# A two-step graph layer on one core: products of the nodes made in the prologue, interleaved keys, lists as a stream, VectorE in text order

## The chip, the core and the metric

The kernel runs on one core of one Trainium2 chip. The metric is device time in microseconds (us); the runs of a kernel are compared by their medians. PE is TensorE (PEld its weight loads), DVE is VectorE, ACT is ScalarE, POOL is GpSimd, SP is SyncE, on whose queue most transfers are issued. L730 is line 730 of the kernel.

## The reference

A graph layer over N = 3327 nodes with 256 features. The matrix `adj` is 3327 x 3327 with about four nonzero entries beside the diagonal in a row.

```python
def _top_p_attention(X, W1, W2, W3):          # 64 wide
    q = X @ W1.T @ W2.T
    k = X @ W3.T
    probs = softmax(q @ k.T)
    ...                                       # keep each row's largest until their sum reaches 0.9
    return A / A.sum(-1, keepdims=True)

h = relu(layernorm(x))
R = adj + eye(N);  R = R / R.sum(-1, keepdims=True)
Z = 0;  Xf = Xa = X = h
for n in range(2):
    A = _top_p_attention(Xa, W1, W2, W3)
    Xf = R @ Xf
    Xa = A @ Xa
    Z = Z + Xf @ U1[n].T + Xa @ U2[n].T
out = x + layernorm(h + Z)
```

## The kernel before

The nodes are cut into NT = 26 tiles of 128 rows. All of h stays on chip (`x0`), as do the keys and queries of a step. A **prologue** makes them: per tile the layer norm, a transposition, and `prep`, which makes keys (L476), rows for moments (L478) and the matrix gsum (L487), in 12 PE instructions of the profile (a matmul of 32-bit numbers is two of them).

Then each of the two steps goes over the 26 tiles, row block by row block, in a software pipeline. For one tile:

- `weights` (L541, L545): logits against all keys in four quarters, exponentials on ACT into a buffer e of 128 x 3328. Its last column goes by way of POOL (L552). `project` (L506 to L525) makes the queries, and on POOL the tile's law, from moments over all keys.
- `measured`: the threshold of the 0.9 mass is guessed from the law and the sum, then corrected by whole passes of ACT over e (L590, 3.08 each), two in step 0 and three in step 1, with small operations on ACT, DVE and POOL between them.
- `settle`: DVE only. The values under the guess (L652), their largest by 20 MAX operations (L656), five or six rounds on the candidates (L661, L663), and the cut itself (L673).
- `Sums.turn` and `Sums.sum`: e is transposed on PE (L717), copied by ACT (L719), and multiplied with the nodes on PE (L730). The last copy (L737) gives the attention row xa.
- `listed`, `packed`, `gathered` (step 0): the nonzero blocks of a row block of `adj`. Seven loads by SP are reduced by DVE (L747), 26 block maxima become a list (L748 to L759); a list's leftovers are packed over the partitions (L764, L777), and POOL gathers five blocks of `adj` (L788) and five of the nodes (L797) by index. In step 0 the blocks are stored (cx) and in step 1 loaded again.
- `spread`: PE multiplies these (L805), which gives Xf; step 1 adds its product at once (L897).
- `first_end` (step 0): the row's Xf and Xa are transposed (L466) and multiplied with U1 and U2 of both steps (L821, L824, L834, 256 wide), since in step 1 R·(Xf U1) and A·(Xa U2) can be summed directly; then `prep` for step 1. `finish` (step 1): the closing layer norm (L842 to L852).

`PLAN` is a table of letters: in each round i of a step, seven parts; each letter advances one piece of a tile's work (m measured, w weights, s spread, e first_end, l lists, f finish), and a part of the sum closes each. `LATE` shifts the sums by parts. At the end PE's and ACT's instructions are tied in the order of this text; DVE's, POOL's and SP's order is left to a scheduler, which sorts by its own model. In round i, settle belongs to tile i, measured to i + 1, weights to i + 2, the sums to i - 1.

`prove` sets a flag where a guess missed, and an exact search behind this code runs only if it is set.

The lists of before stand in the rounds as follows:

```python
for i in range(-3, NT + 2):
    t = i - 1
    if valid(i):
        settle(step, i, live[step, i])
```

```python
def index_next(t):
    if valid(t + 3):
        over[t + 3] = listed(t + 3)
```

Of the kernel before, what the change touches and what calls it, by code (L numbers as in the profile page):

```python
# [9 lines left out]
F32 = mybir.dt.float32  # L10
# [294 lines left out]


# [17 lines left out]
AHEAD = (1, 2)  # L324
CUT = 4
# [13 lines left out]
def guess_graph_layer(ctx, tc, x, adj, w1t, w2t, w3t, u1t, u2t, ln_g, ln_b, out, flag):  # L339
# [22 lines left out]
    x0 = nodes.tile([P, NT, D + 1], F32, tag="x0", name="x0")  # L362
# [10 lines left out]
    for t0 in range(0, NT, 2):  # L373
        nc.sync.dma_start(
            x0[:, t0 : t0 + 2, :D], x[t0 * P : (t0 + 2) * P].rearrange("(t p) d -> p t d", p=P)
        )
# [11 lines left out]
    u1 = const.tile([P, 2, ND, D], F32, tag="u1", name="u1")  # L388
    u2 = const.tile([P, 2, ND, D], F32, tag="u2", name="u2")
    gam = const.tile([P, D], F32, tag="gam", name="gam")  # L390
    bet = const.tile([P, D], F32, tag="bet", name="bet")
    for n in range(2):
        nc.scalar.dma_start(u1[:, n], u1t[n].rearrange("(c p) e -> p c e", p=P))
        nc.scalar.dma_start(u2[:, n], u2t[n].rearrange("(c p) e -> p c e", p=P))
    nc.scalar.dma_start(gam, ln_g.to_broadcast([P, D]))
    nc.scalar.dma_start(bet, ln_b.to_broadcast([P, D]))
    G.memset(x0[:, :, D : D + 1], 1.0)
    for e in es[:4]:
        G.memset(e[:, N:NP], 0.0)
    half = const.tile([P, 2], F32, tag="half", name="half")  # L400
    G.memset(half[:, :1], -0.5)
    G.memset(half[:, 1:], 0.5)
# [26 lines left out]
    ends = const.tile([P, NT], F32, tag="ends", name="ends")  # L429
    index = const.tile([P, NT, DIRECT + 1], I32, tag="index", name="index")  # L430
    hx = dram.tile([P, NT, D + 1], F32, tag="hx", name="hx")
# [29 lines left out]
    def transposed(rows, pt=None):  # L461

        if pt is None:
            pt = ps_t.tile([P, 4, P], F32, tag="pt", name="pt")
        for c in range(ND):
            PE.transpose(pt[:, c, :], rows[:, c * P : (c + 1) * P], ident)  # L466
        xT = tpool.tile([P, ND, P], F32, tag="xT", name="xT", bufs=2)
        S.copy(xT, pt[:, :ND, :])
        return xT


    def prep(step, xT, t):
        h, j = divmod(t, HALF)
# [10 lines left out]
        S.copy(qry[qp, j, :], pk[qp, 0, :])  # L484
        yield
# [6 lines left out]
    def moments(step):  # L492
        gs = small.tile([DA, DA + 1], F32, tag="gs", name="gs", bufs=1)
        V.tensor_scalar(gs, gsum[:, step, :], 1.0 / N, None, ALU.mult)
# [7 lines left out]
    def project(step, t):  # L502
        h, j = divmod(t, HALF)
        qp = slice(DA, P) if h == 0 else slice(0, DA)
        pq = ps_t.tile([P, 4, P], F32, tag="pt", name="pq")
        PE.matmul(pq[:, 0, :], w2d[qp, :], qry[qp, j, :], start=True, stop=True)  # L506
        pr_ = pq[:, 1:3, :].rearrange("p a b -> p (a b)")[:, : 2 * DA + 2]
        PE.matmul(pr_, qry[qp, j, :], qm[qp, step, :], start=True, stop=True)
        qT = tpool.tile([P, P], F32, tag="qT", name="qT", bufs=2)
        S.copy(qT, pq[:, 0, :])  # L510
        mq = small.tile([P, 2 * DA + 2], F32, tag="mq", name="mq", bufs=2)
        S.copy(mq, pr_)
# [8 lines left out]
        G.tensor_tensor(col(2), col(1), half[:, 1:], ALU.pow)  # L521
# [6 lines left out]
    def weights(step, t, live):  # L528

        qT, ms = project(step, t)  # L530
        yield
        e = es[(2, 3, 0, 1, 4, 5)[t % 6] if step else t % 4]
        za = small.tile([P, CUT + 1], F32, tag="za", name="za")
        w = HALF * P
        wd = w // CUT
        for n in range(CUT):
# [11 lines left out]
            else:  # L548
                S.activation(e.rearrange("p (a n) -> p a n", a=2)[:, :, c : w - 1], pl[:, :, : wd - 1],
                             AF.Exp, accum_out=za[:, n : n + 1])  # L550
                S.activation(za[:, n + 1 :], pl[:, 0, wd - 1 : wd], AF.Exp)  # L551
                G.tensor_copy(e[:, w - 1 : w], za[:, n + 1 :])  # L552
        live[step, t] = dict(e=e, za=za, ms=ms, Z=rec[:, step, 3, t : t + 1])
# [5 lines left out]
    def measured(step, r):  # L559
        e, za, ms, Z = r["e"], r["za"], r["ms"], r["Z"]  # L560

        g = small.tile([P, 20], F32, tag="g", name="g")
        r["col"] = col = lambda k: g[:, k : k + 1]
        con = lambda k: one[:, k : k + 1]
        S.activation(za, za, AF.Copy, accum_out=Z)
        S.activation(col(0), Z, AF.Ln)
# [3 lines left out]
        S.activation(col(9), col(3), AF.Exp, scale=ms[:, 3:4], bias=ms[:, 8:9])  # L573
        S.activation(col(4), col(2), AF.Square, bias=con(4))
# [5 lines left out]
        G.tensor_scalar(col(5), col(1), OFFSET[step], None, ALU.mult)  # L580
        if step == 0:
            G.tensor_scalar(col(10), col(9), col(5), 1.0, ALU.mult, ALU.add)
        else:
            G.tensor_scalar(col(14), col(9), 0.25, None, ALU.mult)
        yield
        oa = small.tile([P, 3], F32, tag="oa", name="oa")

        def through(k, f, guess, sign):
            ja = scan.tile([P, NP], U8, tag="ja", name="ja")
            S.activation(ja, e, f, bias=guess, scale=sign, accum_out=oa[:, k : k + 1])  # L590

        through(0, AF.Relu, col(9), -1.0)
        yield
        through(1, AF.Sign, col(12), 1.0)
# [4 lines left out]
        if step == 0:  # L599
            S.activation(col(3), col(4), AF.Square, scale=col(1), bias=con(1))  # L600
            S.activation(col(3), col(3), AF.Ln, scale=0.5, bias=col(10))
            S.activation(col(3), col(3), AF.Identity, scale=-1.0, bias=col(6))
            S.activation(col(3), col(3), AF.Exp, scale=col(11))

            V.tensor_scalar(col(5), oa[:, 1:2], 31.0 - NP, BIG, ALU.is_lt, ALU.mult)
            V.tensor_scalar(col(6), col(4), col(1), 0.35, ALU.mult, ALU.is_lt)
            V.scalar_tensor_tensor(col(5), col(6), BIG, col(5), ALU.mult, ALU.add)
            V.tensor_scalar(col(3), col(3), 1.0e20, col(9), ALU.min, ALU.mult)
            V.tensor_tensor(col(16), col(3), col(5), ALU.add)
            return  # L610
# [405 lines left out]
```

## Time and profile before

| what | value |
|---|---|
| median of 3 runs | 1583.5 us (1581.93 to 1588.3) |
| the profiled execution's own time | 1581.76 us |
| its span in the trace | 1580.0 us |
| busy PE, DVE, ACT, POOL | 88%, 75%, 76%, 53% |
| mean granted TensorE clock | 0.94 |
| step 0, first to last L652 | 115.00 to 837.12 us |
| step 1, first to last L652 | 925.34 to 1527.24 us |

Busy time is an average over stages with different limits, so the stages are read apart: prologue, step 0 with lists, step 0 without, the boundary, step 1, the tail. The granted clock (1.00 is full) tells how fast PE ran in a stage. A row of the chain or of a timeline names engine, line, operation, output and inputs; in brackets stands the idle time ahead of it and what ended it.

### The profile page before, as it was taken

The numbers are of one execution on the slowest core, as the hardware profiler recorded it, in microseconds if no ns is written. First come the engines' busy times: TensorE is split into PE (matmuls) and PEld (weight loads), VectorE is DVE, ScalarE is ACT, GpSimd is POOL, SyncE is SP. The second block draws the span as 40 slices with busy tenths as digits, with TensorE's granted clock in tenths as the row PEclk, the third lists the DMA queues.
The fourth block names the chain that finished last, engine by engine and source line by source line (L and its number), as shares of the span: only waits on it lengthen the run. The fifth ranks groups of instructions, "written<-read, shape, count | busy, mean of one in ns | idle before, by whom it ended". The sixth has DMA issues, their size and how long they took to land.

```text
span 1580.0 us, 23741 instructions
## 1 busy us (share of the span) xinstructions
PE 1389.4 (88%) x6923; PEld 1056.5 (67%) x6923; DVE 1186.5 (75%) x3910; ACT 1203.3 (76%) x2758; POOL 830.6 (53%) x1336
## 2 busy tenths in 40 slices
PE   5967999989999999999999639899989898999885
PEld 4745677767776767777778426676666666766674
DVE  4349887888788777576675058988988889889883
ACT  5457777675776767777774399999999899999961
POOL 6625655456556546556561316556555465565532
PEclk9566999999999999999999859999999999999998
DMA  7623444444545422212221201122121221221210
GB/s 227 174 84 102 129 148 137 139 138 137 156 124 149 138 73 66 65 59 56 61 69 60 61 0 54 58 80 61 61 81 52 69 61 61 80 61 61 80 44 20
DMA packets 86460, 139.64 MB, mean 88 GB/s; under 512 B 14737, under 2 KB 49296, under 8 KB 86320
## 3 DMA queue, kind: packets, MB, share of 16 engines
q1 hardware_dynamic: 67168, 93.76, 19.0%
q0 software_dynamic: 16640, 42.69, 10.1%
q10 hardware_dynamic: 2512, 1.57, 0.3%
q8 instruction: 57, 0.93, 0.2%
q14 instruction: 83, 0.68, 0.1%
HBM read 114.10 MB, written 23.87 MB: 87 GB/s over the span
## 4 chain that ended last, share of the span: by engine, by line
PE 34%; DVE 28%; ACT 16%; DMA 10%; POOL 7%; issue 4%; SPq 0%; POOLq 0%; ACTq 0%; DVEq 0%
PE pa L730 15%; DMA at<-in_adj 7%; ACT ja L590 6%; DVE e L673 5%; DVE cand L656 5%; PE pt L717 5%; PE pr L805 4%; POOL xg L797 4%; PE pl L541 4%; DVE fm L747 4%; DVE w L652 4%; DMA ac<-cx 2%; ACT e L545 2%; PE pk L476 2%; DVE x L673 1%
## 5 line engine op out<-in xcount | busy, mean ns | idle before, releaser
L730 PE MATMUL pa<-xw,eT 128*128 128x256 f32 x1352 | 332.9, 388 | 32.1 <-ACT xa L737 32.1
L719 ACT COPY eT<-pt 128x512 f32<-128x512 f32 (+1 forms) x364 | 202.6, 557 | 190.5 <-PE pt L717 190.5
L730 PE MATMUL pa<-x,eT 128*128 128x256 f32 x1352 | 334.9, 389 | 0.0
L590 ACT ACTIVATE ja<-e,g 128x3328 uint8<-128x3328 f32 x106 | 326.5, 3080 | 0.0
L730 PEld LDWEIGHTS pa<-xw,eT 128*128 128x128 f32 x1352 | 250.2, 191 | 112.5 <-ACT xa L737 41.2
L730 PEld LDWEIGHTS pa<-x,eT 128*128 128x128 f32 x1352 | 255.4, 194 | 34.9 <-issue 1.2
L541 PE MATMUL pl<-k,qT 64*128 64x416 f32 x832 | 210.4, 597 | 51.2 <-ACT qT L510 47.9
L656 DVE MAX8 cand<-w 128x8 f32<-128x168 f32 (+1 forms) x1040 | 248.4, 317 | 0.0
L788 POOL DMA_INDIRECT ac<-in_adj,index x130 | 187.3, 1441 | 97.6 <-DVE index L782 65.4
L717 PE MATMUL pt<-ident,e 128*128 128x128 f32 x1144 | 180.9, 279 | 23.7 <-DVE e L673 9.5
L717 PEld LDWEIGHTS pt<-ident,e 128*128 128x128 f32 x1144 | 140.7, 142 | 66.8 <-ACT xw L835 18.5
L747 DVE TENSOR_REDUCE fm<-at 128x4 f32<-128x512 f32 (+1 forms) x182 | 116.0, 642 | 87.3 <-DMA at<-in_adj 86.7
L673 DVE SCALAR_TENSOR_TENSOR e<-e,rec 128x3328 f32<-128x3328 f32 x44 | 164.3, 3733 | 1.3
L652 DVE SCALAR_TENSOR_TENSOR w<-e,g 128x3328 f32<-128x3328 f32 x44 | 162.1, 3684 | 1.5
L797 POOL DMA_INDIRECT xg<-vx,index x130 | 131.1, 1009 | 54.6 <-issue 34.6
L805 PE MATMUL pr<-xg,ac 128*128 128x257 f32 (+1 forms) x520 | 141.5, 395 | 20.7 <-DVE s L897 20.7
L797 POOL DMA_INDIRECT xg<-hx,index x130 | 127.3, 979 | 35.0 <-issue 32.0
L541 PEld LDWEIGHTS pl<-k,qT 64*128 64x128 f32 x832 | 70.3, 199 | 98.8 <-ACT qT L510 49.6
L552 POOL COPY e<-za 128x1 f32<-128x1 f32 x44 | 21.3, 485 | 212.3 <-ACT za L551 212.3
L545 ACT ACTIVATE e<-pl 128x832 f32<-128x832 f32 x132 | 113.6, 865 | 13.7 <-PE pl L541 13.7
L805 PEld LDWEIGHTS pr<-xg,ac 128*128 128x128 f32 x520 | 90.0, 193 | 35.8 <-DVE s L897 25.0
L577 POOL TENSOR_SCALAR g<-g 128x1 f32<-128x1 f32 x52 | 55.6, 1069 | 84.0 <-ACT g L573 84.0
(217 smaller groups left out, 2326.3 us busy)
## 6 DMA issues: line engine op xcount, KB each, us to landing
at<-in_adj SPq DMA_DIRECT2D x156, 256.0 KB, 3.0
cx<-ac SPq DMA_DIRECT2D x26, 384.0 KB, 2.4
ac<-cx SPq DMA_DIRECT2D x26, 384.0 KB, 3.2
hx<-x SPq DMA_DIRECT2D x26, 128.5 KB, 3.0
x<-in_x SPq DMA_DIRECT2D x13, 256.0 KB, 5.3
at<-in_adj SPq DMA_DIRECT2D x26, 128.0 KB, 2.2
xr<-in_x SPq DMA_DIRECT2D x26, 128.0 KB, 2.2
vx<-sv SPq DMA_DIRECT2D x26, 128.0 KB, 2.1
```

Source lines behind the costliest of these rows:

```text
L541: PE.matmul(pl[:, a, :wd], qT[p, :], keys[step][p].rearrange("p a b -> p (a b)")[:, c : c + wd], start=True, stop=True)
L590: S.activation(ja, e, f, bias=guess, scale=sign, accum_out=oa[:, k : k + 1])
L652: V.scalar_tensor_tensor(w, e, col(16), e, ALU.is_lt, ALU.mult, accum_out=d2)
L656: V.max(cand[:, 8 * s : 8 * s + 8], w[:, s * SEG : min(NP, (s + 1) * SEG)])
L673: V.scalar_tensor_tensor(e, e, at(1), e, ALU.is_ge, ALU.mult, accum_out=ra)
L717: PE.transpose(pt[:, j, :], e[:, (j0 + j) * P : (j0 + j + 1) * P], ident)
L719: S.copy(eT[:, :w, :], pt[:, :w, :])
L730: PE.matmul(self.pa, eT[:, j - 4 * k, :], self.xa[:, j, :D], start=j == 0, stop=j == NT - 1)
L747: V.tensor_reduce(fm[:, j0 : j0 + n], at[:, :n], AX.X, ALU.max, apply_absolute_value=True)
L788: G.indirect_dma_start(out=ac[:, k, :], out_offset=None, in_=rows, in_offset=bass.IndirectOffsetOnAxis(ap=index[:, t, k : k + 1], axis=0), ...
L797: G.indirect_dma_start(out=xg[:, k, :w], out_offset=None, in_=rows, in_offset=bass.IndirectOffsetOnAxis(ap=index[:, t, k : k + 1], axis=0))
L805: PE.matmul(pr[:, :w], ac[:, k, :], own if k == KT - 1 else xg[:, k, :w], start=k == 0, stop=k == KT - 1)
```

## The change

1. **Products once.** The product of h with U1 of both steps (512 wide) is made in the prologue by a new `products`, 11 tiles there and the rest in the first two rounds, and stored in `ax` (step 0's half) and `bx` (step 1's half, with a column of ones). R is applied to these rows instead of to h: `spread` of step 0 diffuses `bx`, adds `ax` scaled, and stores `vx` itself. `first_end` keeps only xa's transposition and one 512-wide product with U2.
2. **Interleaved keys.** Tile t of keys lies at column block t // 2 of half t % 2. So three quarters of the key columns need only the first tiles, and the weights of tiles 0 to 2 of each step are begun before the last keys are there: in the prologue, and in rounds 24 to 26 of step 0. The moments leave the last tiles uncounted.
3. **Lists as a stream.** `listed` becomes one generator over all tiles, a unit being one load with its reduce: two units per prologue tile from t = 6, then six per round.
4. **Order of DVE.** `settle` is cut into seven pieces, with letters d (and c, n for the pieces carried into the next round); the new letters a, p, g stand for lists, packing and gathering. DVE's instructions are now tied in text order too. LATE is one part larger in both steps.
5. **Step 1's measurement.** Eight small ACT operations between the passes go; some of their work moves to DVE, more to POOL; DVE's small operations after the third pass fall from 13 to 8 in all. The last column's exponential is written and summed by ACT itself.

```diff
-        h, j = divmod(t, HALF)
+        j, h = divmod(t, 2)
...
-                S.activation(za[:, n + 1 :], pl[:, 0, wd - 1 : wd], AF.Exp)
-                G.tensor_copy(e[:, w - 1 : w], za[:, n + 1 :])
+                S.activation(e[:, w - 1 : w], pl[:, 0, wd - 1 : wd], AF.Exp, accum_out=za[:, n + 1 :])
...
+        V.tensor_scalar(col(3), oa[:, 1:2], float(NP), col(7), ALU.add, ALU.mult)
+        V.tensor_scalar(col(4), col(3), oa[:, 0:1], 0.0, ALU.subtract, ALU.max)
...
+        G.tensor_scalar(col(12), col(4), d1, col(1), ALU.subtract, ALU.mult)
+        G.tensor_scalar(col(8), col(8), col(12), None, ALU.mult)
+        G.tensor_scalar(col(12), col(12), col(12), 1.0e-12, ALU.mult, ALU.add)
+        G.tensor_tensor(col(12), col(12), half[:, 2:], ALU.pow)
+        G.tensor_scalar(col(12), col(12), col(8), 0.7, ALU.mult, ALU.max)
+        G.tensor_scalar(col(11), col(12), 1.5, col(11), ALU.min, ALU.mult)
...
-    def first_end(t, xf, xa):
-        fT = transposed(xf)
-        yield
-        aT = transposed(xa)
+    def first_end(t):
+        aT = transposed(live.pop(("r", t)))
         yield
         pz = ps_r.tile([P, 2 * D], F32, tag="pr", name="pz")
...
         for c in range(ND):
-            PE.matmul(pz[:, D:], fT[:, c, :], u1[:, 1, c, :], start=c == 0, stop=c == ND - 1)
-        sv = row.tile([P, 2 * D], F32, tag="sv", name="sv", bufs=2)
-        S.copy(sv, pz)
-        nc.sync.dma_start(vx[:, t, :], sv[:, D:])
...
+            PE.matmul(pz, aT[:, c, :], u2[:, c].rearrange("p n d -> p (n d)"), start=c == 0, stop=c == ND - 1)
+        S.copy(xw[:, t, :], pz[:, D:])
...
+    def products():
+
+        for t in range(NT):
+            pool, tag = ((ps_a, "pa"), (ps_r, "pr"))[t % 2]
+            pz = pool.tile([P, 2 * D], F32, tag=tag, name="pz")
+            for c in range(ND):
+                PE.matmul(pz, hT[:, t, c, :], u1[:, c].rearrange("p n d -> p (n d)"),
+                          start=c == 0, stop=c == ND - 1)
+            u = uh[:, t % 4, :]
+            (V.tensor_copy if t < EARLY[1] else S.copy)(u[:, : 2 * D], pz)
+            nc.sync.dma_start(ax[t], u[:, :D])
+            nc.sync.dma_start(bx[:, t, :], u[:, D:])
+            yield
...
+        if t >= 6:
+            run(lister, 2)
+            if t % 2 == 0:
+                run(product, 1)
...
+        own = row.tile([P, D + 1], F32, tag="own", name="own", bufs=2)
+        nc.sync.dma_start(*((own[:, :D], vx[:, t, :]) if step else (own, bx[:, t, :])))
+        s1 = row.tile([P, D], F32, tag="s1", name="s1", bufs=4)
+        nc.sync.dma_start(s1, (sx if step else ax)[t])
...
         V.scalar_tensor_tensor(s1, pr[:, :D], rr, s1, ALU.mult, ALU.add)
-        live["f", t] = s1
...
+        if step == 0:
+            nc.sync.dma_start(vx[:, t, :], s1)
...
-    PLAN = (("mwsss", "lmsss", "ewl", "wee", "mee", "mwel", "we"),
-            ("mwss", "lms", "ww", "mssf", "mw", "msf", "mw"))
-    LATE = (0, 3)
...
+    PLAN = (("mdwsssa", "mdsssa", "ewpda", "wsda", "mpdea", "mwedga", "wmdeg"),
+            ("cmwss", "cnms", "wwnfd", "mdsss", "smwdfg", "mdfg", "mwdf"))
+    LATE = (1, 4)
...
-    for engine in (PE.engine, S.engine):
+    for engine in (PE.engine, S.engine, V.engine):
```

What this does to the order is seen at three places. First DVE in step 0, before, ahead of one tile's settle: the reduces of a list (L747) and its small operations stand in one clump between the operations that end `measured` (L605 to L609).

```order
L747 TENSOR_REDUCE fm<-at 128x2
L747 TENSOR_REDUCE fm<-at 128x4
L748 SCALAR_TENSOR_TENSOR fm<-fm,back 128x26
L749 MEMSET fm 128x1
L751 MAX lists<-fm 128x8
L752 MATCH_REPLACE fm<-lists,fm 128x26
L754 TENSOR_SCALAR index<-lists 128x4
L753 MAX lists<-fm 128x8
L747 TENSOR_REDUCE fm<-at 128x4 x2
L605 TENSOR_SCALAR g<-oa 128x1
L828 TENSOR_TENSOR sv<-sv,x_95 128x256
L747 TENSOR_REDUCE fm<-at 128x4 x2
```

The same engine and step now, inside a settle (L708 to L727 are its rounds and its cut; the settle of the next tile is L696):

```order
L881 TENSOR_TENSOR sv<-pz,x_95 128x256
L800 TENSOR_REDUCE fm<-at 128x4
L723 SCALAR_TENSOR_TENSOR e_101,ra<-e_101,rec 128x3328
L724 RECIPROCAL ra<-ra 128x1
L800 TENSOR_REDUCE fm<-at 128x4
L626 TENSOR_SCALAR g<-oa 128x1
```

The reduces (now L800) stand singly between long operations, and the end of `measured` comes after the cut.

Second, DVE in step 1, before, from the cut (L673) to the next tile's settle: the small operations after the third pass (L628 to L641) come in one row behind the cut.

```order
L673 SCALAR_TENSOR_TENSOR x_95,ra<-x_95,rec 128x3328
L675 TENSOR_TENSOR cum<-dr,bb 128x48
L674 RECIPROCAL ra<-ra 128x1
L897 SCALAR_TENSOR_TENSOR s_11542<-pr,rrs,s_11542 128x256
L676 TENSOR_REDUCE rec<-cum 128x1
L628 TENSOR_SCALAR g<-g 128x1
L629 TENSOR_TENSOR g<-g 128x1
L630 TENSOR_SCALAR g<-g 128x1
L639 TENSOR_SCALAR g<-g 128x1
L631 TENSOR_SCALAR g<-g 128x1
L632 RECIPROCAL g<-g 128x1
```

And now, from y's scaling (L895, formerly L849) over the cut (L723) to the next settle (L696):

```order
L895 TENSOR_SCALAR s_10734<-s_10734,mv,rstd 128x256
L723 SCALAR_TENSOR_TENSOR x_95,ra<-x_95,rec 128x3328
L724 RECIPROCAL ra<-ra 128x1
L537 SCALAR_TENSOR_TENSOR mq,ms<-mq 128x64
L726 TENSOR_TENSOR cum<-dr,bb 128x48
L727 TENSOR_REDUCE rec<-cum 128x1
L679 TENSOR_SCALAR g<-oa 128x1
L680 TENSOR_SCALAR g<-g 128x1
L681 SCALAR_TENSOR_TENSOR g<-g 128x1
L682 TENSOR_SCALAR g<-g 128x1
L696 SCALAR_TENSOR_TENSOR w,d_11494<-e_102,g 128x3328
```

Four small operations are left there; L662 and L663 stand earlier, among the rounds, and L670 to L675 are POOL's.

Third, PE at the boundary of the steps, before: after the last products (L834) and keys (L476 to L487) come moments (L496), projections (L506, L508) and all logits (L541).

```order
L834 MATMUL pw_8740<-u_133,xT 128x256 x2
L476 MATMUL pk<-xT,wk 128x128 x2
L478 MATMUL pk<-wk,xT 128x64 x2
L487 MATMUL pg<-krs 64x65
L496 MATMUL pq<-gs,w2x 128x65
L506 MATMUL pq<-qry,w2d 128x128
L508 MATMUL pq<-qm,qry 128x130
L541 MATMUL pl<-k_98,qT 128x416 x8
```

And now: moments (L509) and the laws of three tiles (L525) stand among the last sums (L782), and behind the last products (L878) and keys come six logits (L563), the last quarters of three tiles.

```order
L782 MATMUL pa<-x_95,eT 128x256 x4
L509 MATMUL pq<-gs,w2x 128x65
L525 MATMUL pq<-qm,qry 128x130 x3
L865 MATMUL pr<-xg,ac 128x257 x3
L782 MATMUL pa<-x_95,eT 128x256 x2
L865 MATMUL pr<-xg,ac 128x257 x2
L865 MATMUL pr<-own,ac 128x257
L475 MATMUL pt<-ident,xa 128x128 x2
L878 MATMUL pz<-u_133,xT 128x512 x2
L486 MATMUL pk<-xT,wk 128x128 x2
L488 MATMUL pk<-wk,xT 128x64 x2
L563 MATMUL pl<-k_98,qT 128x416 x6
```

433 lines of the change are left out of this document (241 added, 192 removed).

## Prediction

> **What bounds the kernel now.** I read the page first, for busy shares and the chain that ended last:
>
> ```profile
> PE 1389.4 (88%) x6923; PEld 1056.5 (67%) x6923; DVE 1186.5 (75%) x3910; ACT 1203.3 (76%) x2758; POOL 830.6 (53%) x1336
> PE 34%; DVE 28%; ACT 16%; DMA 10%; POOL 7%; issue 4%; SPq 0%; POOLq 0%; ACTq 0%; DVEq 0%
> ```
>
> TensorE is busiest, yet only a third of the chain: the limit changes hands, so I cut the span into stages. A tile's settle begins with one long DVE operation, L652 (26 in each step). The first and last of each step, from DVE's timeline:
>
> ```profile
> 115.00 3.68 DVE L652 SCALAR_TENSOR_TENSOR w<-e,g 128x3328 f32<-128x3328 f32 x1
> 837.12 3.68 DVE L652 SCALAR_TENSOR_TENSOR w<-e,g 128x3328 f32<-128x3328 f32 x1
> 925.34 3.68 DVE L652 SCALAR_TENSOR_TENSOR w<-e,g 128x3328 f32<-128x3328 f32 x1
> 1527.24 3.68 DVE L652 SCALAR_TENSOR_TENSOR w<-e,g 128x3328 f32<-128x3328 f32 x1
> ```
>
> So: prologue 115.0; 25 periods of step 0, 722.1 (mean 28.9); boundary 88.2; 25 periods of step 1, 601.9 (mean 24.1); tail 52.8. Next, busy time by stage (columns: span, then busy PE, PEld, DVE, ACT, POOL with instructions, granted clock, DMA share, GB/s):
>
> ```profile
> 0.00:115.00 115.00, 83.42 (x365) 62.87 (x365) 42.02 (x140) 61.38 (x202) 59.84 (x175) 0.69 0.56 164
> 54.00:90.00 36.00, 34.52 (x146) 28.38 (x145) 7.26 (x19) 13.90 (x63) 15.99 (x26) 0.50 0.42 120
> 115.00:189.10 74.10, 58.21 (x260) 41.37 (x260) 66.40 (x232) 53.43 (x124) 46.30 (x60) 0.82 0.40 119
> 343.10:465.80 122.70, 114.55 (x579) 87.07 (x577) 101.60 (x342) 85.47 (x204) 68.48 (x96) 0.97 0.48 140
> 643.00:671.20 28.20, 27.80 (x146) 21.30 (x144) 18.97 (x65) 21.40 (x52) 16.87 (x24) 1.00 0.21 61
> 837.10:882.80 45.70, 45.70 (x254) 39.81 (x253) 20.72 (x70) 15.10 (x38) 3.27 (x5) 1.00 0.14 45
> 882.80:925.30 42.50, 17.93 (x78) 10.61 (x77) 3.43 (x21) 27.03 (x64) 15.89 (x32) 0.70 0.17 47
> 1065.50:1089.60 24.10, 21.88 (x112) 16.43 (x111) 21.59 (x70) 23.11 (x51) 13.45 (x22) 1.00 0.22 67
> 1527.20:1580.00 52.80, 34.82 (x184) 29.95 (x182) 24.70 (x76) 9.05 (x17) 11.35 (x14) 0.89 0.06 17
> ```
>
> Row 4 is four tiles while neighbour lists are made, 30.7 each; row 5 is one tile after the last list, full PE. Between them lie the lists: L747 reduces blocks of the matrix on DVE, seven per list, and six lists fall into row 4. The waits there (250 to 560; total, times, longest), the load, the first and last reduces of two stretches of the prologue, and, for later, two quarters of a tile's logits on PE at half clock:
>
> ```profile
> DVE fm L747 <- DMA at<-in_adj: 48.9, 43, 3.0
> at<-in_adj SPq DMA_DIRECT2D x156, 256.0 KB, 3.0
> 24.80 1.26 DVE L747 TENSOR_REDUCE fm<-at 128x4 f32<-128x512 f32 x2
> 70.92 0.42 DVE L747 TENSOR_REDUCE fm<-at 128x2 f32<-128x256 f32 x1 [0.42 <-DMA at<-in_adj]
> 92.90 0.67 DVE L747 TENSOR_REDUCE fm<-at 128x4 f32<-128x512 f32 x1
> 113.65 0.69 DVE L747 TENSOR_REDUCE fm<-at 128x4 f32<-128x512 f32 x1 [0.75 <-DMA at<-in_adj]
> 907.69 3.15 PE L541 MATMUL pl<-k,qT 64*128 64x416 f32 x8 [11.60 <-ACT qT L510]
> ```
>
> DVE in row 4: 101.6/4 = 25.4 busy, and 48.9 over ten tiles is 4.9 waiting, together 30.3 of the 30.7. So DVE with its lists sets those periods, PE the later ones. In the prologue 21 reduces start 2.3 apart, 13 later ones 1.73.
>
> **Part 1, prologue (term T1).** It gains the products h·U1, three tiles' first three quarters of logits, and 44 reduces instead of 34 ahead of the settle; with six more in round -1, 50 stand ahead of the first settle (now L696). At 2.0 each from 24.8 that is 125 (bounds 1.73 and 2.3: 111 and 140). PE is not last at full clock: by row 2 a prologue tile has 12 instructions and costs 34.52 x 12/146 = 2.84 at half clock; with 11 products (four 512-wide instructions, 3.4; priced in part 2) and nine quarters (3.15/2) the 26 tiles make some 126 at half, about 63 at full. The copies of products are DVE's, but the reduces wait on loads anyway. **T1 = +10.**
>
> **Part 2, step 0 (T2).** Per tile it drops the two transposes of Xf and replaces sixteen 256-wide instructions by four 512-wide:
>
> ```profile
> 849.37 0.38 PE L466 MATMUL pt<-ident,xa 128*128 128x128 f32 x2
> 849.59 1.03 PE L821 MATMUL pz<-u,xT 128*128 128x256 f32 x4
> 850.45 1.89 PE L730 MATMUL pa<-x,eT 128*128 128x256 f32 x8
> ```
>
> From start to start, two transposes take 0.22 and four 256-wide 0.86, so 0.215 each; a 512-wide one I take at twice that, 0.43. PE: 27.8 - 0.22 - 3.44 + 1.71 = 25.8. DVE: 18.97 (row 5), plus 6/7 of a list at 25.4 - 18.97 = 6.4 per 1.5 lists and some 1.3 more for the pieces around it, 4.7 in all; +0.46 for Xf scaled and added on DVE instead of ACT; +0.8 of gaps: 24.9. Two engines this close wait on each other now and then; I add 0.5 to the larger: 26.3. The first three periods stay at 74.1 (row 3), since loads and clock, not PE's work, made them. T2 = 74.1 + 22 x 26.3 - 722.1 = **-69**; bounds 25.8 (-80) and 27.6 (-41), the second where PE's and DVE's saving is half lost. ACT (21.4) loses two copies. The new loads and stores of ax and bx are three per tile of 128 KB, beside a DMA share of 0.2 to 0.5; they cost nothing while that is free, and stand on SP's queue ahead of matrix loads (rival 1).
>
> **Part 3, boundary (T3, T4).** Lists no longer end there, but sums come a part later, and three tiles' first weights are issued among the last sums: nine quarters at 0.79, 7.1 in all, and some 1 of early diffusion, less 4 for two tiles' products: 45.7 becomes 49.8, **T3 = +4**. Then, from the last attention row to step 1's first settle, the chain is ACT's:
>
> ```profile
> 888.96 0.26 ACT L484 COPY qry<-pk 64x128 f32<-64x128 f32 x1
> 904.76 0.21 ACT L568 ACTIVATE za<-za 128x5 f32<-128x5 f32 x1 [8.06 <-POOL e L552]
> 907.70 3.07 ACT L590 ACTIVATE ja<-e,g 128x3328 uint8<-128x3328 f32 x1
> 918.68 3.05 ACT L590 ACTIVATE ja<-e,g 128x3328 uint8<-128x3328 f32 x1
> ```
>
> The 8.06 was a wait on POOL's one-column copy, which ACT's accumulation now replaces. From the rows: last keys 882.8 to 889.2, 6.4 less 2.2 for PE work gone; a last quarter, 2.3; L568 to the first pass 2.9 less 0.6; two passes 6.5; the small operations to the third pass 3.2; that pass 3.3; from there to the settle 3.5, +0.5 for more of it on POOL. Sum 25.8, with 1.2 for other tiles' quarters 27: **T4 = -15.5** (-18.5 if the chain shrinks to 24; -7 if only the 8.06 goes and a microsecond comes back).
>
> **Part 4, step 1 (T5).** A steady tile, DVE's timeline and waits (1041 to 1186, six tiles):
>
> ```profile
> 1080.45 0.41 DVE L849 TENSOR_SCALAR y<-y,mv,rstd 128x256 f32<-128x256 f32 x1 [1.57 <-POOL rstd L458]
> 1087.17 0.20 DVE L628 TENSOR_SCALAR g<-g 128x1 f32<-128x1 f32 x1
> 1089.25 0.27 DVE L641 TENSOR_SCALAR g<-g 128x1 f32<-128x1 f32 x1 [0.35 <-ACT g L637]
> 1089.56 3.69 DVE L652 SCALAR_TENSOR_TENSOR w<-e,g 128x3328 f32<-128x3328 f32 x1
> DVE y L849 <- POOL rstd L458: 9.4, 6, 1.6
> PE pa L730 <- ACT xa L737: 8.8, 6, 1.5
> PE pr L805 <- DVE s L897: 4.5, 6, 0.8
> 915.48 0.29 ACT L596 ACTIVATE g<-oa,g 128x1 f32<-128x1 f32 x1
> 915.81 0.39 ACT L597 ACTIVATE g<-oa,g 128x1 f32<-128x1 f32 x1
> ```
>
> Nothing is idle for long: ACT 23.1 busy and almost no wait, DVE 21.6. ACT loses eight small operations at 0.33 apart (last two rows), -2.65, and gains an accumulator read, 0.2: from 23.7 to 21.3. DVE loses the 1.57 (y is scaled later in its order) and the 2.39 from 1087.17 to 1089.56, and gets eight small operations back, 1.75: 21.9. PE's own demand is 24.1 - 1.5 - 0.8 = 21.9. All three meet at 21.9; +0.6 for meeting: 22.5. **T5 = 25 x 22.5 - 601.9 = -39**; bounds 21.9 (-54) and 23.3 (-19). POOL has 13.45 of 24.1 and takes nine operations more (0.2 to 0.6 each, some 2.2), hidden unless they are held up:
>
> ```profile
> 1067.32 1.93 POOL L577 TENSOR_SCALAR g<-g 128x1 f32<-128x1 f32 x1 [2.65 <-ACT g L573]
> 1069.31 0.22 POOL L578 TENSOR_SCALAR g<-g 128x1 f32<-128x1 f32 x1
> ```
>
> The same one-column operation takes 1.93 where it starts beside DVE's long L652, and 0.22 right after that ends. The new chain (L670 to L675) waits for DVE's L663 and runs near the long L723; caught, it costs 2.2 + 3.6 = 5.8, and DVE's way round it from one settle to the next stays under 21.9, so I leave the sum. The Trainium skill, "SBUF — State Buffer", section "Who interferes with whom", says that a DVE operation with two SBUF inputs and a GpSimd one that reads SBUF exclude each other for a whole instruction, which speaks against putting small operations on POOL. The 1.93 against 0.22 agrees; by that rule the step could pay up to 3.6 per tile, which is rival 2.
>
> **Tail (T6).** Sums end a part later than before, half hidden: **+1.5**.
>
> **Sum:** 10 - 69 + 4 - 15.5 - 39 + 1.5 = -108 on a span of 1580.0, so 1472; the profiled execution took 1581.76, so 1474. The median shown, 1583.5, is 1.7 above that execution, which I leave out.
>
> **Rivals.** 1, slower: DVE stalls at reduces. Its order is now the text's, so a late load stops the settle behind it. SP's queue is in order, and stores that wait for DVE (vx, sx) stand ahead of matrix loads. Six reduces stand in a tile: period 24.9 + 6w, w the mean wait. Break-even is a period of 26.3 + 108/22 = 31.2, w = 1.05; the waiting reduces of before waited 48.9/43 = 1.14, so it is near. At w = 1.5, 33.9, 7.6 more than 26.3, gives 1474 + 22 x 7.6 = 1641. Against it: the reduces stand about 4 apart with two buffers, so a load has some 8 for its 3.0.
> 2: step 1 meets badly, POOL's chain held behind DVE's long operations or five gathers: periods 23.3 to 24.0, +20 to +37, about 1500.
> 3: PE's clock. In row 2 it was granted 0.50 although PE was busy 34.5 of 36. From 33 on at half, 17 tiles (48), 11 products (37), nine quarters (14) and the first settle's passes with their small operations (14) reach 146, 21 later than T1: about 1495. The Trainium skill, "TensorE: Matmul & The Clock Gate", Part 1, says that a sustained busy window of about 3.4 us brings the full clock; the row differs, so the rule would make this rival void, and the row keeps it alive.
> 4: a guess misses and the exact search behind runs: milliseconds more.
>
> **Chances.** Forecast 0.58; rival 1 0.08; rival 2 0.19; rival 3 0.14; rival 4 0.01. Under 0.5% could not be told from no change here. Rivals 2 and 3 still end 5% faster, so faster 0.90; the weak part of rival 1, with w near 1.05, is the same, 0.03, and the rest slower, 0.07. All good bounds (T1 -4, T2 -80, T4 -18.5, T5 -54) give 1431; all bad ones without rival 1 (T1 +25, T2 -41, T4 -7, T5 -19) give 1546. They hardly fall together on the bad side, and 512-wide instructions might cost less than I take: 1425 to 1535.
>
> **What would show it.** T1: the first L696 at 125, reduces 2.0 apart until then. T2: periods of 26 with PE without idle; if DVE waits on at more than 1 us per reduce, rival 1. T4: 27 from the last attention row of step 0 to the next L696, no 8 us hole in ACT. T5: periods of 22.5; if ACT waits on POOL's exponent (L675), rival 2. A granted clock at 0.5 until 130 is rival 3. The prediction is wrong if step 0's period stays at 28 or more, or step 1's at 24.

## The result and the profile after

The changed kernel took 1519.36 us (median of 4 runs, 1517.55 to 1520.27) against 1585.38 for the kernel before: a ratio of 0.9583, 95% interval 0.9558 to 0.9608. The profiled execution took 1517.55, its span is 1515.8. So it is 66 us faster; 108 had been forecast. The first lines of the page and its chain:

```profile
PE 1347.6 (89%) x6657; PEld 991.4 (65%) x6657; DVE 1228.7 (81%) x3824; ACT 1119.9 (74%) x2529; POOL 1010.8 (67%) x1516
ACT 32%; PE 25%; POOL 23%; DVE 10%; issue 7%; DMA 2%; SPq 0%; ACTq 0%; POOLq 0%; DVEq 0%
```

PE and ACT lost work as planned. POOL's busy time rose by 180, and POOL now carries 23% of the chain instead of 7%. The same landmarks as before, the first long DVE operation of a settle (now L696), give the stages, in us:

| stage | before | forecast | after | change forecast | change measured |
|---|---|---|---|---|---|
| prologue, to the first settle | 115.0 | 125 | 135.0 | +10 | +20.0 |
| step 0, 25 periods | 722.1 | 653 | 656.0 | -69 | -66.1 |
| last settle of step 0 to its last attention row | 45.7 | 49.8 | 54.6 | +4 | +8.9 |
| from there to step 1's first settle | 42.5 | 27 | 29.6 | -15.5 | -12.9 |
| step 1, 25 periods | 601.9 | 562.5 | 584.5 | -39 | -17.4 |
| tail | 52.8 | 54.3 | 56.1 | +1.5 | +3.3 |

Busy time by stage of the changed kernel (columns as in the prediction): the prologue and a stretch of it, five tiles of step 0 while lists run, one tile at the end of step 0, five tiles of step 1.

```profile
0.00:135.00 135.00, 102.73 (x461) 61.29 (x461) 64.38 (x201) 71.23 (x227) 54.52 (x175) 0.92 0.60 178
54.00:90.00 36.00, 36.00 (x206) 24.34 (x206) 15.58 (x47) 20.97 (x80) 8.05 (x17) 0.97 0.53 153
317.20:449.20 132.00, 128.62 (x652) 94.93 (x651) 120.47 (x382) 100.61 (x245) 83.79 (x115) 1.00 0.45 131
764.70:791.00 26.30, 25.64 (x132) 19.36 (x131) 19.50 (x62) 20.05 (x49) 14.97 (x18) 1.00 0.28 79
1010.35:1128.50 118.15, 108.76 (x552) 82.59 (x550) 106.05 (x321) 104.44 (x211) 103.89 (x151) 1.00 0.23 68
```

Step 0 is PE's now: 128.62/5 = 25.7 of 26.4 per tile, and with lists or without it the period is the same. Step 1 takes 23.6, with PE at 21.8 and POOL at 20.8.

**Prologue.** What stood ahead of the first settle (L630, the last small operation of `measured`), and when ACT had its part of it (L623) done:

```profile
117.84 0.29 ACT L623 ACTIVATE g<-g 128x1 f32<-128x1 f32 x1
120.55 14.29 PE L920 MATMUL pz<-u,xw 128*128 128x512 f32 x28 [9.62 <-DVE e L923]
126.29 0.69 DVE L923 COPY e<-pz 128x512 f32<-128x512 f32 x1 [1.23 <-PE pz L920]
130.99 0.42 DVE L800 TENSOR_REDUCE fm<-at 128x2 f32<-128x256 f32 x1 [1.69 <-DMA at<-in_adj]
133.63 0.69 DVE L800 TENSOR_REDUCE fm<-at 128x4 f32<-128x512 f32 x1 [0.94 <-DMA at<-in_adj]
134.85 0.16 DVE L630 TENSOR_TENSOR g<-g 128x1 f32<-128x1 f32 x1
135.04 3.69 DVE L696 SCALAR_TENSOR_TENSOR w<-e,g 128x3328 f32<-128x3328 f32 x1
```

ACT was ready at 118.1. DVE, in text order, first had to copy products (L923) and reduce blocks (L800) whose loads came late, and PE waited 9.62 for those copies.

**Step 1.** POOL's rows beside DVE's two long operations, and the waits over seven tiles (963 to 1128):

```profile
986.74 3.68 DVE L696 SCALAR_TENSOR_TENSOR w<-x,g 128x3328 f32<-128x3328 f32 x1
986.93 3.63 POOL L642 TENSOR_SCALAR g<-g,ms 128x1 f32<-128x1 f32 x1
1004.64 3.68 DVE L723 SCALAR_TENSOR_TENSOR x<-x,rec 128x3328 f32<-128x3328 f32 x1
1004.52 3.89 POOL L675 TENSOR_SCALAR g<-g 128x1 f32<-128x1 f32 x1
ACT g L677 <- POOL g L675: 9.9, 7, 1.4
DVE g L662 <- POOL g L655: 6.6, 7, 1.0
```

Two operations on one column, 0.25 and 0.30 long when alone, lie on POOL until the long DVE operation ends. That agrees with the rule of the Trainium skill, "SBUF — State Buffer", section "Who interferes with whom". L642 comes before the gathers on POOL's queue, so these and L655 start 3.4 later and DVE's L662 waits; L675 makes ACT wait 1.4 with the next tile's first pass behind it. From 986 to 1010 POOL's rows follow one another with no gap longer than 0.3: POOL is full here.

**The boundary.** From the third pass of the first tile:

```profile
867.59 0.19 ACT L596 ACTIVATION_READ_ACCUMULATOR ja<-e,g 128x1 f32 x1
869.24 0.94 POOL L857 DMA_INDIRECT xg<-vx,index  x1 [0.30 <-issue]
870.43 0.27 POOL L655 TENSOR_SCALAR g<-g 128x1 f32<-128x1 f32 x1
870.74 0.27 DVE L662 TENSOR_SCALAR g<-oa,g 128x1 f32<-128x1 f32 x1 [7.29 <-POOL g L655]
871.30 0.39 ACT L665 ACTIVATE g<-g,one 128x1 f32<-128x1 f32 x1 [3.52 <-DVE g L663]
```

The old hole of 8 is gone. In its place is one of 3.5: a small POOL operation (L655) that DVE needs stands behind step 1's gathers, the last of which is L857 here.

### The profile page after: what moved, and what is told of

The parts are those of the page before. It is cut to its first block, busy times and chain, and to the rows that moved or that the text cites. A ratio compares the mean times of both kernels' runs of the same rounds, so it can differ in the third digit from the quotient of the medians.

```text
span 1515.8 us, 23135 instructions
## 1 busy us (share of the span) xinstructions
PE 1347.6 (89%) x6657; PEld 991.4 (65%) x6657; DVE 1228.7 (81%) x3824; ACT 1119.9 (74%) x2529; POOL 1010.8 (67%) x1516
## 3 DMA queue, kind: packets, MB, share of 16 engines
q1 hardware_dynamic: 78400, 104.00, 22.4%
## 4 chain that ended last, share of the span: by engine, by line
ACT 32%; PE 25%; POOL 23%; DVE 10%; issue 7%; DMA 2%; SPq 0%; ACTq 0%; POOLq 0%; DVEq 0%
ACT ja L596 14%; PE pa L782 12%; POOL xg L857 8%; POOL g L675 5%; ACT eT L770 5%; PE pl L563 4%; PE pt L768 4%; ACT e L567 3%; DVE cand L701 2%; PE pz L920 1%; DVE cand L710 1%; DVE w L696 1%; DVE e L723 1%; DMA at<-in_adj 1%; DVE bb L708 1%
## 5 line engine op out<-in xcount | busy, mean ns | idle before, releaser
L782 PE MATMUL pa<-xw,eT 128*128 128x256 f32 x1352 | 331.2, 387 | 30.9 <-ACT xa L789 30.6
L782 PE MATMUL pa<-x,eT 128*128 128x256 f32 x1352 | 334.1, 389 | 0.0
L782 PEld LDWEIGHTS pa<-xw,eT 128*128 128x128 f32 x1352 | 249.8, 191 | 103.4 <-ACT xa L789 46.3
L848 POOL DMA_INDIRECT ac<-in_adj,index x130 | 197.5, 1520 | 139.4 <-DVE index L841 106.1
L782 PEld LDWEIGHTS pa<-x,eT 128*128 128x128 f32 x1352 | 250.4, 191 | 59.8 <-issue 29.0
L768 PE MATMUL pt<-ident,e 128*128 128x128 f32 x1144 | 179.2, 277 | 47.0 <-DVE e L723 31.6
L563 PE MATMUL pl<-k,qT 64*128 64x416 f32 x832 | 199.6, 562 | 10.4 <-ACT qT L528 9.9
L865 PE MATMUL pr<-xg,ac 128*128 128x257 f32 (+1 forms) x520 | 144.4, 401 | 22.5 <-DVE s L974 20.0
L857 POOL DMA_INDIRECT xg<-bx,index x130 | 136.7, 1052 | 38.8 <-issue 28.7
L696 DVE SCALAR_TENSOR_TENSOR w<-e,g 128x3328 f32<-128x3328 f32 x44 | 161.9, 3679 | 0.7
L723 DVE SCALAR_TENSOR_TENSOR e<-e,rec 128x3328 f32<-128x3328 f32 x44 | 161.8, 3678 | 0.1
L857 POOL DMA_INDIRECT xg<-vx,index x130 | 127.8, 983 | 41.4 <-issue 35.9
L800 DVE TENSOR_REDUCE fm<-at 128x4 f32<-128x512 f32 (+1 forms) x182 | 115.5, 637 | 40.6 <-DMA at<-in_adj 40.2
L865 PEld LDWEIGHTS pr<-xg,ac 128*128 128x128 f32 x520 | 91.1, 195 | 39.7 <-DVE s L974 20.3
L563 PEld LDWEIGHTS pl<-k,qT 64*128 64x128 f32 x832 | 67.0, 188 | 52.2 <-issue 37.1
L708 DVE MAX8 bb<-cand 128x8 f32<-128x160 f32 x286 | 92.8, 325 | 6.4
L675 POOL TENSOR_SCALAR g<-g 128x1 f32<-128x1 f32 x26 | 83.2, 3202 | 2.8
```

What stands on the lines that cost most here:

```text
L563: PE.matmul(pl[:, a, :wd], qT[p, :], keys[step][p].rearrange("p a b -> p (a b)")[:, c : c + wd], start=True, stop=True)
L696: V.scalar_tensor_tensor(w, e, col(16), e, ALU.is_lt, ALU.mult, accum_out=d2)
L723: V.scalar_tensor_tensor(e, e, at(1), e, ALU.is_ge, ALU.mult, accum_out=ra)
L768: PE.transpose(pt[:, j, :], e[:, (j0 + j) * P : (j0 + j + 1) * P], ident)
L782: PE.matmul(self.pa, eT[:, c - 4 * k, :], self.xa[:, j, :], start=c == 0, stop=c == NT - 1)
L848: G.indirect_dma_start(out=ac[:, k, :], out_offset=None, in_=rows, in_offset=bass.IndirectOffsetOnAxis(ap=index[:, t, k : k + 1], axis=0), ...
```

## The experiments

Each is an edit of the changed kernel. e1, e3, e4 and e5 ran on one chip, c1, e8, e9 and e10 on a second, c2, e11 and e12 on a third, e13 on a fourth; which chip the first comparison ran on is not known. Each chip had one series only, so what is said below of a chip could also lie in the hour. Theory A was that POOL sets step 1's period, its rival B that POOL's time is hidden.

**One operation off POOL (e1).**

```diff
-        G.tensor_scalar(col(11), col(12), 1.5, col(11), ALU.min, ALU.mult)
+        yield                                  # and one more letter m, ahead of the cut
+        V.tensor_scalar(col(11), col(12), 1.5, col(11), ALU.min, ALU.mult)
         yield
```

> Only the last operation of step 1's POOL chain (L675) goes to DVE, right ahead of the cut. Theory A (POOL's operations caught beside DVE's two long ones, and what queues behind them, set step 1's period of 23.6): POOL loses 3.9 of its 20.75 busy per tile, ACT's wait of 1.42 for it goes, period 22.2 to 22.7, the whole 22 to 35 us shorter than the changed kernel's 1519. Theory B (PE, ACT and DVE, each at 21 to 22, only meet badly; POOL's time is hidden): period 23.4 to 23.8, time within 5 us of 1519.

Measured: 1598.09 (step 0 was slower in this series, 726.8; see the control below), period 23.52 in step 1. Theory A's number missed and B's (23.4 to 23.8) came, but POOL's rows give another reason than B's:

```profile
1061.06 3.64 POOL L642 TENSOR_SCALAR g<-g,ms 128x1 f32<-128x1 f32 x1
1078.96 4.22 POOL L898 TENSOR_TENSOR s<-s,gam 128x256 f32<-128x256 f32 x1 [0.39 <-DVE s L896]
1060.90:1178.80 117.90, 109.06 (x554) 82.48 (x550) 105.67 (x325) 104.80 (x211) 102.17 (x147) 1.00 0.23 68
```

With L675 gone, POOL's next operation with SBUF inputs (L898, the closing norm's scaling) is the one caught beside the cut, for 4.22, and L642 is caught as before. POOL's sum hardly changes (102.2 in five tiles against 103.9), and neither does the period.

**Both caught operations and their neighbours off POOL (e3).** As e1, and L639 to L643 become DVE operations ahead of L650.

> As e1, and the five one-column operations at the start of step 1's measurement (L639 to L643, one of them caught for 3.63 beside L696) also go to DVE, between the halves of its MAX operations. Theory A: POOL's gathers start some 3.4 earlier after the settle's start and DVE's wait of 0.94 at L662 goes; period 22.0 to 22.4, a further 0 to 10 us gained. Theory B: DVE's busy time rises from 21.2 to some 22.4, period 23.6 to 24, no gain.

The whole took 1583.64, with step 0 slow again (736.0). Period 22.78: 0.83 per tile less than the changed kernel's 23.61, though DVE has six operations more. It is above the 22.0 to 22.4 expected, but B's 23.6 to 24 is out. With the same step 1 code, in a later kernel (e12), four tiles and the chain of one:

```profile
1019.20:1110.30 91.10, 87.00 (x442) 66.00 (x440) 86.65 (x281) 83.58 (x169) 68.87 (x96) 1.00 0.24 70
by line: POOL xg L858 21.5%; POOL s L898 18.6%; DMA xr<-in_x 18.3%; issue 10.9%; POOL xr L897 9.0%; DVE bb L709 4.0%; DVE cand L711 3.5%; POOL s L899 3.2%; POOL ms L541 2.5%; POOL ms L545 1.7%; SPq L902 1.5%; POOL ms L540 1.5%; DVE s L896 1
```

POOL is down to 17.2 per tile, yet the chain still goes round POOL: gathers, the caught L898, and the load of xr, whose only buffer is free when the addition behind that scaling (L899) has ended. The 22.8 is read as that loop, since PE has only 21.75; no run with a second buffer tests it.

**No lists in round -1 (e4).**

```diff
-                a=lister if step == 0 and i else none,
+                a=lister if step == 0 and i > 0 else none,
```

> Round -1 of step 0 makes no list units (they follow in the later rounds). Theory C (the first settle waits at 135 because DVE, in text order, has reduces with late loads and product copies ahead of the small operations that ACT had ready at 118): first L696 at 121 to 125, the whole 8 to 14 us shorter. Rival D (the seven products with PE at half clock hold it, the lists do not): first L696 at 130 or later, 0 to 4 us gained.

```profile
122.69 3.69 DVE L696 SCALAR_TENSOR_TENSOR w<-e,g 128x3328 f32<-128x3328 f32 x1
```

The first settle comes at 122.69 against 135 to 136. That is theory C's range, and D falls, since the products are still there. The time of this run (1589.10) hides it: its step 0 took 738.6, for the reason that the control shows.

**DVE without text order (e5).** `V.engine` is left out of the list of tied engines.

> DVE is left to the scheduler again; all else as in the changed kernel. If the text order on DVE brought step 0's periods from 30 to 26.4: they go back to 28 or more, total 40 us or more longer. If the stream of lists and the smaller PE work did: periods stay at 26 to 27, the prologue gets some 10 us shorter, step 1 moves within 1 us per tile, total within 1500 to 1530.

It took 1666.85. The prologue is shorter (first settle 122.1). Step 0's 25 periods take 669 (122.1 to 790.9), with 26 to 30 while lists run and 26.3 afterwards: against 656 in the changed kernel's first profile. The second theory's step 0 and prologue came, but neither its step 1 nor its total. So of the 66 gained in step 0 the text order brought about 13 (e13 below gives the same step 0 in another series); the rest came with the other parts (less PE work, lists spread over the rounds), which were not taken apart further. Step 1 goes to 30 per tile:

```profile
ACT g L665 <- DVE g L663: 27.8, 4, 7.0
```

The scheduler put the two small operations L662 and L663 behind the cut, and ACT waits 7.0 per tile for them. In step 1 the text order is what makes the period.

**The control (c1): the changed kernel again, unaltered.**

> The changed kernel itself, unaltered, beside the experiments. Theory E (step 0 has two courses for the same program: PE without idle keeps the full clock and 26.4 per tile; one late ACT or DVE instruction makes PE idle, the clock falls for a 3.4 us window, and the lateness goes on, 26 to 34 per tile): either near 1519 with no clock dip in step 0, or near 1590 with one dip per tile or two, as in e1 and e4, whose step 0 is the same instruction by instruction. Rival F (something in e1, e3 and e4 made their step 0 longer): 1519 here.

It took 1612.18 (ratio 1.0165, interval 1.0111 to 1.0220): on this chip the same program is slower than the kernel before, which itself took 1584.11. Prologue (136.3), boundary (86.1) and step 1 (23.6) agree within 2 us; nearly all of the difference, 94.6 of 99.8 in the span, is step 0's 750.6 instead of 656.0. One tile of step 0 of the control, and one of the first profile, then step 0 as a whole, in the same order:

```profile
425.40:459.40 34.00, 30.98 (x140) 22.05 (x139) 24.16 (x79) 21.40 (x55) 16.71 (x23) 0.90 0.36 100
136.30:886.90 750.60, 663.57 (x3098) 480.75 (x3099) 587.14 (x1868) 491.02 (x1183) 405.11 (x546) 0.93 0.38 109
422.70:449.20 26.50, 25.77 (x132) 19.03 (x131) 24.45 (x79) 20.13 (x49) 16.75 (x23) 1.00 0.44 128
135.00:791.00 656.00, 622.34 (x3098) 457.20 (x3099) 586.26 (x1869) 491.34 (x1183) 408.94 (x545) 0.98 0.43 124
```

The granted clock fell for one window of 3.4 us, sometimes two, in nearly every tile from 242 on, and not once between 190 and 790 in the first profile. PE is busy 41 longer for the same instructions, and idle 53 longer. What starts it can be read where ACT copies a block that PE has transposed. First the control, then the first profile:

```profile
233.45 0.60 PE L768 MATMUL pt<-ident,e 128*128 128x128 f32 x4
236.29 0.59 ACT L770 COPY eT<-pt 128x512 f32<-128x512 f32 x1 [1.24 <-PE pk L488]
236.93 0.39 PE L833 MATMUL po<-lists,oh 128*128 128x13 f32 x2 [0.95 <-ACT eT L770]
230.32 0.60 PE L768 MATMUL pt<-ident,e 128*128 128x128 f32 x4
231.01 0.58 ACT L770 COPY eT<-pt 128x512 f32<-128x512 f32 x1
```

The transposition ends at 234.05 and the copy starts 2.2 later, where it took 0.09 in the first profile. The trace also holds the semaphore updates: in step 0 of the first profile none of PE's comes more than 0.03 after the matmul's end. In the control 65 of the 548 of step 0 are missing, so not all can be paired with their matmuls; paired as early as their order allows, one in six comes over 0.36 late. In the stretch above all pair off: the update of the product before (L878, ended at 231.88) comes 2.8 late, that of the transposition 2.2, and the next three follow within 0.2. (The 1.9 in the next expectation is too low.) PE then waits for the copy, and in the following windows the clock falls. So the course is theory E's, but what comes late is PE's own signal and not an ACT or DVE instruction, and the time is 22 over the 1590 expected. That the lateness goes on because PE, at 97% of the period, cannot recover is argued, not shown. The Trainium skill, "TensorE: Matmul & The Clock Gate", Part 1, gives a free-running window of some 3.4 us for the clock; the lengths here (3.4 and 6.8) agree. The kernel before took 1583 to 1584 in both series with late updates. Its step 0 with lists was bounded by DVE, with PE idle in every tile; but from 580 to 805, behind its lists, PE was busy 221.79 of 225.00 in its first profile, and its time was no longer in these series. Whether its signals are late there was not seen, since neither trace of it comes from them. The second:

> The kernel before, unaltered, for its trace on this chip. In the changed kernel's slow executions PE's semaphore updates reach the trace up to 1.9 us after the matmul's end, while POOL's gathers run, and in its quick one never over 0.03. Theory G (the signals are late on this chip for any kernel, but DVE-bound step 0 of before has slack): the same late updates here, step 0's periods with lists at 30 to 31 as before, time within 1% of 1583. Rival H (only the changed kernel's order brings them about): no late updates here.

It took 1582.80, with no late update and periods of 30 to 31 with lists. But no run of this series has late updates, so between G and H nothing is decided. A trace at hand narrows it: e5 ran in a series with late updates, and while its lists ran 26 of 310 recorded ones came over 0.36 late. Behind its last list (569) it was 1 of 175, with no fall of the clock, though POOL's gathers went on and PE was busy 98%:

```profile
585.00:790.90 205.90, 200.99 (x1017) 148.52 (x1017) 150.21 (x507) 158.19 (x380) 133.43 (x181) 1.00 0.29 79
```

So gathers and a full PE together are not enough. In the control 8 of 40 were still late behind its last list; what makes the difference is not known.

**More distance between transposition and sum (e10).** `AHEAD = (2, 2)`.

> AHEAD of step 0 is 2 instead of 1: PE's transpositions and ACT's copies of them run two parts ahead of the sum that uses them. If PE idles because ACT's copy for the next sum comes late (theory E), the extra part covers a lateness of some 3 us: period 26 to 27 without dips, 1500 to 1525. If PE then waits for DVE's cut instead (it ends 24.1 after the settle's start, the transposition would come at 23 to 24): period 27 to 29, no gain.

It took 1649.67, on the control's chip, 37 slower than the control; step 0 took 779.9, 31.2 per tile, outside both theories' ranges. From 440 to 790 PE waits for DVE's cut in nearly every tile, as the second theory had it, and the clock is 0.92. But PE's larger wait is another:

```profile
PE po L833 <- ACT eT L770: 24.4, 11, 2.5
PE pt L768 <- DVE e L723: 11.7, 10, 2.3
440.00:790.00 350.00, 308.49 (x1430) 222.98 (x1430) 264.18 (x843) 221.49 (x545) 183.64 (x253) 0.92 0.39 109
```

This wait for the copy is some 2 per tile, as in the control (31.4 in 15 waits from 440 on). L833 writes to one of the two buffers that also take the transposed blocks, so it has to wait for a copy however far ahead the blocks are made. So e10 left in place the wait that it was to remove, and does not test theory E.

**POOL in text order too (e8), and with e3 (e9).** `G.engine` is added to the tied engines, and the gathers of step 1's tile 1 come one round later.

> POOL's instructions are tied in text order as well, and of step 1's first gathers only those of tile 0 come before the first settle. Theory A with the queue: the five gathers (6 us) no longer stand ahead of L655 to L657, so the hole of 3.5 on ACT at the boundary goes (from the last attention row of step 0 to the first settle of step 1 26 instead of 29.6), and step 1's period falls from 23.6 to about 23, with L675 still caught. If POOL's order is worse in text order: step 1's period 24 or more, or step 0's gathers late and its period over 28.

> e3 (the cut's and the settle's neighbours on DVE) and e8 (POOL in text order, fewer gathers first) together. Theory A: step 1's period 22.0 to 22.5, boundary 26, so 35 to 45 shorter than the unaltered changed kernel beside it. Theory B: step 1 stays at 22.8 as in e3 or is longer.

They took 1648.13 and 1662.50. In e8 the boundary did not shrink (86.7 from settle to settle), and step 1 went to 25.4: ACT now waits 3 us a tile for L675 (five tiles):

```profile
ACT g L677 <- POOL g L675: 15.5, 5, 3.8
```

In e9 step 1 took 25.1 to 26.5. In step 1 the scheduler's order on POOL was the better one; the queue at the boundary stays a reading of the profile, not shown by a run. Ahead of it the text order was better: e8's first settle came at 128.1 instead of 136.3 in the control, and its second period took 25.1 instead of 31.5, though its whole step 0 was no shorter (749.8).

**No gathers in step 0 (e11).** Two fills with zeros in place of ten gathers, so that Xf is left out.

> The changed kernel with step 0's ten gathers per tile by POOL left out (two buffers are filled with zeros instead, so Xf is wrong; attention, lists, PE's and DVE's work are as before). Theory G: the late signals in step 0 are gone with the gathers, PE does not idle, no clock dips, period 26.4 or a little less, step 0 656 or less, whichever chip. If late signals come from something else (the matrix loads, the stores): periods of 27 to 34 as in the unaltered one on such a chip.

```profile
131.80:781.40 649.60, 620.69 (x3098) 454.88 (x3099) 582.41 (x1869) 491.59 (x1183) 165.22 (x351) 0.99 0.30 88
```

It took 1500.73, step 0 649.6. But no run on this chip has late signals, so this tells only what POOL's gathers (165 busy here against 409) cost step 0 where signals are on time: nothing in a steady tile, and 7.8 in the second period, which took 23.8 instead of 31.6. The changed kernel's first profile shows how (SP's wait between 150 and 190, DVE's reduce, PE's wait between 154 and 186):

```profile
SPq L970 <- DMA ac<-in_adj,index: 23.0, 1, 23.0
171.98 0.69 DVE L800 TENSOR_REDUCE fm<-at 128x4 f32<-128x512 f32 x1 [7.65 <-DMA at<-in_adj]
PE pt L768 <- DVE e L723: 8.8, 1, 8.8
```

The store of the gathered blocks (L970) waits for a gather, matrix loads stand behind it on SP's queue, the settle's reduce waits for one of them, and PE for the cut; in e11 PE's wait for that cut is 1.3. Whether the gathers make PE's signals late stays open: in the control's step 0, 52% of the matmuls with a late update ended while POOL issued a gather, against 37% of all that can be paired, which is a leaning in time and no more.

**The best of both (e12).** e3 and e4 together.

> e3 (the two caught operations and their neighbours to DVE) and e4 (no list units in round -1) together. By the stages of e3 and e4: first settle at 122.5 instead of 136, step 1's period 22.8 instead of 23.6, so 32 shorter than the unaltered changed kernel on the same kind of chip: 1485 to 1490 where step 0 runs at 26.4, near 1565 to 1580 where it has late signals and dips.

It took 1490.03, ratio 0.9405 (0.9361 to 0.9449), as expected: first settle 121.4, step 0 657.7, step 1 22.8 per tile. It is quicker than the kernel before beside it and than the changed kernel's 1519.36, which is from another series; signals were on time in both.

**Text order on DVE in step 1 alone (e13).**

```diff
-        queue = [i for i in trace[begin:] if i.engine == engine]
+        queue = [i for i in trace[later if engine == V.engine else begin:] if i.engine == engine]
```

`later` is the place in the text where step 1 begins; the rest is e3.

> e3, with DVE tied in text order in step 1 alone; in the prologue and step 0 the scheduler orders it, instruction by instruction as in e5. By the stages of e5 (first settle 122.1; step 0's 25 periods 669, on a chip with late signals, without a clock dip) and of e3 (step 1 569 in 25 periods), boundary 84 and tail 56: some 1500 where signals are late, and 1485 to 1495 where they are not, since step 0 is bounded by PE either way. If the scheduler's order on DVE brings back the periods of 30 of the kernel before while lists run: 1540 or more. If text order from the boundary on does not bring step 1 to 22.8: 1550 or more.

It took 1505.21, ratio 0.9441 (0.9405 to 0.9478), with no late update on its chip; somewhat over the 1485 to 1495 expected for that case. (The kernel before took 1598.20 beside it.) Step 0 took 668.8 (122.7 to 791.5), as in e5, where signals were late: this order costs 11 to 13 against the text's where signals are on time, and in e5's series it was 58 to 70 quicker than the text's (726.8 in e1, 736.0 in e3, 738.6 in e4).

## Why the prediction was right, and where not

The range held the time and the sign was right; the likeliest value was 45 too low, and the gain 66 instead of 108. Half of the miss is step 1, where by the prediction's own sign (ACT waits for L675) it was rival 2 that came, given 0.19. That the range held also took luck: in the control's series the same kernel took 1612, outside it and no gain.

- **T2 (step 0) was right by its working.** PE's demand was worked out as 25.8 and is 25.7, the period forecast as 26.3 is 26.4 with lists; the whole miss lies in the first three periods, 78.0 instead of 74.1. Rival 1, late loads in DVE's order, cost next to nothing in the steady rounds (DVE waited 0.9 for matrix loads in five tiles), but it came once: the 7.65 in the second period, behind the store of gathered blocks (e11). One sum is off: 6/7 of 6.4/1.5 and 1.3 make 5.0, not 4.7, so DVE's demand would be 25.2 instead of 24.9. PE's 25.8 stays the larger; DVE's measured 24.1.
- **T1 had the right queue and too short a time.** The 50 reduces did stand ahead of the first settle, 2.28 apart (21.8 to 133.6) instead of 2.0. Among the last six, DVE waited 4.3 for products that it had to copy, which the sum had put at nothing. It also took the queue as given: ACT's guess was there at 118. Taking the list units out of round -1 alone brought the settle to 122.7 (e4), the scheduler's order to 122.1 (e5).
- **T3 and T4** were too low by 5 and 2.6. For T3 PE was busy 53.8 of the 54.6, so the stretch is its work: diffusion (L865) took 8.5 from start to start instead of 5.2, with 1 more counted, and projections and laws (L509 to L525) 3.0, with none counted; for T4 the term "0.5 for more of it on POOL" left out that a queue of gathers stands ahead of that POOL work: 3.5 of ACT waiting.
- **T5 was mis-sized: 17 gained, 39 forecast.** The step that failed is "DVE's way round it from one settle to the next stays under 21.9, so I leave the sum". The loop was priced for L675 alone, and across DVE; the loop that binds is POOL's own: gathers, small operations, two of them caught for 3.6 and 3.9. POOL's demand, 13.45 and 2.2 in the prediction, came to 20.8. PE (21.8), ACT (20.9) and DVE (21.2) stayed within the 21.9 that the term gave them. Rival 2 named this mechanism and priced it at 23.3 to 24.0; 23.6 came. e3 shows that the caught group was worth 0.83 per tile, e1 that one operation of it is worth nothing, since the next takes its place.
- **Rival 3 (half clock) did not come**: the granted clock was 0.97 in the stretch where it had been 0.50, with PE busy all of it.
- **T6** was 3.3 instead of 1.5; why was not looked into.
- **What no term had**: that step 0 in this order depends on PE's signals' being on time. The control shows a price of 95, in step 0 alone, enough to turn the gain into a loss.

## What to carry to other kernels

Price a queue, not only an operation: when work moves to an engine with room, list what stands behind it there and what long operation it can be caught beside, since taking out one caught operation only hands its place to the next. Text order pays where a consumer would otherwise be put behind a long operation (step 1), and costs where it holds a ready chain behind loads (the prologue); it can be chosen by stage. A gain in a stage packed as closely as this should be measured on more than one chip before it is believed.

## What the runs showed of the hardware

- The same program took 1519 us in one series and 1612 in another; PE's semaphore updates were late there, by 2.8 in the rows shown, in step 0 above all. The kernel before showed no difference between the two series (1585 and 1584). Why the signals are late is open; gathers and a full PE together do not always bring it about (1 late of 175 behind e5's lists).
- With late signals more than the waiting was lost: in the control's step 0 the clock was at half for 106 us instead of 20, mostly 3.4 or 6.8 at a time, and of the 95 lost PE's longer work is 41. From 190 on, no gap of PE there is longer than 2.7 (first profile: 0.9 up to 860).
- A matmul 512 wide started every 0.43 (L878 at 226.88, 227.31, 227.74, 228.17 in the first profile), as taken from the 256-wide ones at 0.215.
